# A two-block convolution network on one core: the second block's 3x3 convolution in tiles of four by four

## The chip, the cores and the metric

The kernel runs on one core of a Trainium2 chip. The time is that of one launch on the device, in microseconds (us); the median of several runs is given, and one further execution is profiled. The engines work side by side, each through its own queue in order, and wait for one another by semaphores: PE multiplies matrices (its weight loads are shown as PEld), DVE and ACT work element by element, POOL does a little, and SP issues most transfers. All data are 32-bit floats.

## What is computed

Eight images of 512 channels and 32 by 32 pixels pass two layers, each behind a group norm and added to its input. The first layer holds nearly all the work. Cut to what matters:

```python
t = cbs(x, cv1_w, cv1_bn, 0)            # 1x1, 512 -> 512
ys = [t[:, :C], t[:, C:]]               # C = 256
for i in range(N):                      # two blocks
    yi = ys[-1]
    z = cbs(yi, m_cv1_w[i], m_cv1_bn[i], 1)      # 3x3, 256 -> 256
    z = bot_attention(z, m_qkv_w[i], m_rw[i], m_rh[i])
    z = jax.nn.silu(bn_eval(conv2d(z, m_cv2_w[i], 0), m_cv2_bn[i]))
    ys.append(yi + z)
return cbs(jnp.concatenate(ys, axis=1), cv2_w, cv2_bn, 0)   # 1x1, 1024 -> 512
```

Here cbs is convolution, batch norm and SiLU. The attention has four heads of 64 channels over the 1024 pixels, with learned position terms added to the keys. The second layer is a depthwise 3x3 convolution (nine taps for each channel), ReLU, a threshold for each channel, a 1x1 convolution 512 to 512, ReLU and a threshold. The change concerns the 3x3 convolution of the second block.

## The kernel before, in words

**Pieces and lists.** Each step of an image is cut into small pieces, put under short names in a table (`add`, line 306), and four written lists say in which order the pieces are issued (`go`, line 309): FIRST (line 45) for image 0, then for each later image HEAD (line 63) followed by TAIL (line 79), or by LAST (line 85) for image 7. A list thus runs from one image into the next: HEAD begins with the 1x1 convolution of its own image (c, y) and also ends the second layer of the image before (o, O with ok, ou, oa and their capitals; fr, f). As every engine but POOL is bound to program order (`InOrder`), a list fixes the order on PE, DVE, ACT and SP.

**The names used below.** In a block: d, P, Rc, R, B, E, Ez are the 3x3 convolution; k, ka, kd, q, qa, v, va make keys, queries and values; s, e, p, w are the steps of attention (scores, exponentials, running sums, values), h, z, n, nr, ns, sc its end (n sums on PE, nr the reciprocal, ns eight transfers that spread it over the channels, sc the rescaling of z); m, ma, mr are the closing 1x1 convolution with its residual. o and O are products of the 1x1 convolution of the second layer, t the depthwise taps, Q the products of the last 1x1 convolution of the first layer, r0 to r3 sums of its right sides. ta, ti and to, in FIRST alone, transform the 3x3 weights once and write them to DRAM; rl and `ring_load` read them back.

**The 3x3 convolution** (`conv3`, line 737, used for both blocks) is done by a Winograd method in tiles of four columns by two rows: 6 by 4 = 24 products for each tile of eight outputs, in place of 72. The image is stored by column phase (x modulo four), padded, in `yp` (line 194). On DVE, `along_rows` (line 758) combines the columns and `across_rows` (line 786) the rows, which gives for each of three pairs j of column components four row components of 512 elements (128 channels of a half, in kr, vt and qy, which are free then). `products` (line 803) multiplies: for each j and each half m of the outputs, one piece P of 4 x 2 x 2 matmuls, 128 by 128 weights with 128 moving columns:

```python
for c in (1, 2, 0, 3):
    for i in range(2):
        at = place[c] * 256 + i * P
        for k in range(2):
            nc.tensor.matmul(
                flat(ps)[:, at : at + P],
                u[:, i, c, k, :],
                component(j, c)[:, (2 * i + k) * P : (2 * i + k + 1) * P],
                start=(k == 0), stop=(k == 1),
            )
```

Rc (ACT) copies one component out of PSUM, R (`rows_back`, line 822) turns the four components back on DVE, reading the rest from PSUM, B and E (lines 845, 865) do the columns, and Ez (line 870) applies the batch norm and SiLU into z.

**Weights and buffers.** A piece P takes one tile of 1 MB from the ring of `NRING` = 5 buffers (line 147) and asks for the next load at its end. Tiles of all kinds go through the ring in the order of use (`ring_sources`, line 387): for one block of a later image two tiles for o and O (or for cv1), six u tiles of the convolution, the qkv weights. A tile of o or O stays until its seventh product is done. Temporary tiles of 1024 elements come from a pool of `NWORK` = 11 (line 145).

Of the kernel before, what the change touches and what calls it, by code (L numbers as in the profile page):

```python
# [10 lines left out]
F32 = mybir.dt.float32  # L11
# [16 lines left out]
PITCH = F // 4 + 1  # L28
NWORK = 11
# [17 lines left out]
    ca ta2*2 c rl ca ta1*3 ti2 ti1 to1 d ti1 d y ya to1 ti1 y ya ti2 to2 d ti2 d to2 rl d*2 y ya  # L47
    y ya P*2 Rc R Rc d dw d*3 R d*2 P Rc P*3 Rc R B*2 R B Rc R E Ez B Rc R E Ez ta0 k*3 ka kp k X
    ka q*4 ta0*2 qa*2 v ti0 to0 ta1*2 to0 s e ti0*2 kp ta1 v va v*2 va ti1 s ti1*2 w s*2 e*2 w s
    e*2 p*3 w s*2 p ta2 e w*2 to1 e s*2 w p*2 s e p e w to1 e w ta2 s h p z e ta2 s e w*2 p s*2  # L50
    ti2 e*2 p w to2*2 s e s w*2 e p w*2 ti2*2 s*2 e*2 w p*2 s*2 w h e w s e w s e p s w s e*2 p*5
    n nr p z rh ns e p nc sc s e w*2 s*2 w*2 e*2 s w s*2 w h s z w sc e*4 w p*4 s w*2 e w p*2 w
    nc p n dp h z S nr nc*2 ns sc*2 Q m ma K mr m ma m*2 ma*2 mr*2 Q K mr d*7 P*2 Rc R d P Rc R
    Rc d*2 R d P Rc d R B*2 P Rc R E B P Rc Ez R B E Ez k cw rk X k*3 ka kp ka kp cw*3 v*2 va v*2
    va q rk q qa q cw s e cw q qa s e p w s*2 e p e p w cw s*2 dx w e p s e p e s e p*2 w*3 s e w
    g s e w h z s*2 e w s e w s g*2 s w p s*2 e*2 cw e cw w*2 e s p*2 w*2 s*2 cw w p*2 e p e*3 rk
    p cw*2 h p s z e s e w s e w rk p g p w*2 p w s n p nr s*2 e ns p*2 sc e w e nc s*2 g*3 e w s
    e*2 s e p w h s e nc w s e g p*3 w*3 p*2 w*3 sc w p h z*2 Q S n nr nc ns sc Q gm m ma mr sc
    m*3 ma*2 mr*2 ma mr Q u Q A x gd u Q A x gv i gp nc i*3 Q im id Q iv ip ib b gb A x bm i ga*4
    t i t*3 ct Q ct Q A x i*2  # L60
# [3 lines left out]
    c*4 ck cu ct*2 ca cu t im c cu*2 c*2 id iv cu y ca t cu*2 ca yk ca y*2 ip y t*2 d yu d ya y  # L64
    ib yu d*2 P d yu d*2 b P Rc R b bm d P d*2 y Rc R Rc b d R d B P Rc l B lr R B P Rc R E B P
    Rc R E Ez*2 yu bm*2 y lp yu ya yu*2 k t*19 v*2 va k*2 ya*2 ka k ka v*2 va X l kd q*2 qa lr lp
    t kd q s e t q qa s e p w s e s e p w*2 s*2 e*2 w s*2 w*2 s e*2 w s w e*2 s p*5 h e l w s*2 w
    e*2 lr t s w*2 p*2 e s e s e t w s w*2 z e s*2 e w e s w s*2 h e p e w s*2 p*5 z w e*3 s*2 e
    t w e p*2 s*2 e*2 w*2 l lr w p ot s p*2 e p*3 lp w h z n nr nc ns p*2 w lp w s*2 w e s w*2
    e*2 w*3 p sc p sc nc S p ot h z n nr o ok o ns O Ok ou oa ot*2 O sc m sc ma m ma Ou Oa m mr  # L70
    ma m ma O o mr*3 Ou ou d o d ou o O*2 d*2 P Ou ou Ou d*2 o ou d Rc ou nc R oa d*2 Ou oa P Rc
    d nc O P R d*2 P Rc P R B Oa Rc P R Ou Oa B*2 Rc B Rc R E R E Ez*2 o O k*4 ou oa Ou Oa ka*2
    fr*3 v*2 va q*2 v*2 dp qa g va g q X kd f g f kd s e q qa fr f*2 dx s e w s*2 e w e s*2 w s*2
    e*4 p*2 w s g*3 p*3 g s w*2 e s w*2 e*2 s*2 w g h s w e*2 w p*4 s*2 w s*2 w p*2 s*2 e p w e*6
    p w*2 h s*2 e*2 z p*4 w p*2 s e s z e w p*2 s n nr ns e w*4 nc s nc s e w p e w h s*2 w sc w
    e w s*2 e*3 w s p e p sc p*4 w*4 z n h z nr S ns
# [3 lines left out]
    r2 r0 Q*3 r0 sc*2 r0*2 m*2 r1 m ma gm m nc gd ma gv r1 ma r3 mr*2 K mr r2 r3 gp r2 ma mr r1  # L80
    gb ga r1 K ga ct r2 Q r3 Q*4 u1 u0 r3 Q u0*4 Q u0 Q a1 Q a0 x0 a0 ga x0 i a0 x0 i*3 im u0 a0
    id x1 ga ct Q iv ip Q u1 x0 ib b i u1 i bm t u1 t Q*2 u1 t*2 u1*2 a1 x1 a1*2 x1*2 i*2 nc
# [3 lines left out]
    Q*2 nc sc m sc nc rg m*3 ma*3 mr ma mr*3 Q A Q x i*2 im id Q iv ip Q ib Q A x b bm i*2 t*2 im  # L86
    id Q iv t*2 ip t*2 ib t b bm t*2 Q A x i*2 t Q l lr lp t im id t Q A iv ip t Q ib b bm t*4 x
    t A x t i*2 l lr o*2 t im id o iv t lp ip t ib o*2 rg b bm t*4 l lr t lp t*5 l lr lp o*20 oa
    o oa o*6 fr f oa*2 fr f oa*2 fr f oa*2 fr f
# [34 lines left out]
def fast_kernel(  # L124
# [54 lines left out]
    def load(dst, b):  # L179
# [14 lines left out]
    yp = [const_tile([P, 4, 2, F, PITCH], f"yp{l}") for l in range(2)]  # L194
# [9 lines left out]
        [dram.tile([P, 2, 4, 2, P], F32, tag=f"u{l}_{i}", name=f"u{l}") for i in range(6)]  # L204
        for l in range(2)
# [44 lines left out]
    for t in yp:  # L250
        nc.gpsimd.memset(t, 0.0)
# [5 lines left out]
    sc12 = const_tile([P, 4], "sc12")  # L257

    def fold_norms():
# [11 lines left out]
        nc.vector.tensor_scalar(sc12, sc[:, BN2 : BN2 + 4], -1.0 / 12.0, None, ALU.mult)  # L271
# [26 lines left out]
    def inner(t, m):  # L298
        return t[:, :, m, :, : F // 4]
# [19 lines left out]
    PAIRS = ((1, 2), (3, 4), (0, 5))  # L319

    def transform_weights(l, outer_queue):
# [26 lines left out]
        def store(j, c, t, queue=nc.sync):  # L348

            for m in range(2):  # L350
                src = t.rearrange("p (i m x) -> p i m x", i=2, m=2)[:, :, m]
                dst = u_dram[l][2 * j + m][:, :, c].rearrange("p i k o -> p i (k o)")
                queue.dma_start(dst, src)
# [16 lines left out]
        def outer_rows(j, c, dy):  # L370
            t = planes.pop((j, dy))
            nc.scalar.mul(t, t, 2.0)
            store(j, c, t, outer_queue)

        return (
            [[lambda j=j, dy=dy: along_rows(j, dy) for dy in range(3)] for j in range(3)],
            [[lambda j=j, i=i: inner_rows(j, i) for i in range(3)] for j in range(3)],
            [
                [lambda j=j, c=c, dy=dy: outer_rows(j, c, dy) for c, dy in ((0, 0), (3, 2))]
                for j in range(3)  # L380
            ],
# [5 lines left out]
    def ring_sources():  # L387
        for b in range(B):
            for l in range(2):
# [3 lines left out]
                for i in range(6):  # L393
                    yield u_dram[l][i].rearrange("p a b c d -> p (a b c d)"), 2048
# [288 lines left out]
    def cv1(order):  # L683
# [17 lines left out]
        def first_end(m):  # L701
            act(inner(yp[0], m - 2), by_phase(flat(open_.pop(m))), AF.Silu, BN0 + m)
# [21 lines left out]
    def quartered_cv1():  # L724
# [4 lines left out]
        def end(ps, p, low, n):  # L729
            m = 2 * p + low  # L730
            dst = inner(yp[0], low) if p else phases(y0[:, m, :])
            act(dst[:, :, n * 16 : n * 16 + 16], by_phase(ps), AF.Silu, BN0 + m)
# [4 lines left out]
    def conv3(l):  # L737
# [3 lines left out]
        yf = yp[l].rearrange("p r k h t -> p (r k h t)")  # L741
# [128 lines left out]
        def close(m):  # L870
            n = 2 * l + m
# [5 lines left out]
                scale=sc12[:, n : n + 1],  # L877
# [15 lines left out]

    def positions(l, m):
# [5 lines left out]
        nc.vector.tensor_tensor(phases(t), col.to_broadcast(full), row.to_broadcast(full), ALU.add)  # L900
        nc.sync.dma_start(r_dram[l][:, m], t)

    def qkv(l, by_input):


        wt, tiles, values = [], {}, {}
# [6 lines left out]
        def products(m, k):  # L913
            w = weights()
            if m not in tiles:
                tiles[m] = big_tile("ps_qk")
            for n in range(2):
                nc.tensor.matmul(
                    tiles[m][:, n, :],
# [8 lines left out]
        def keys(m):  # L928
            nc.scalar.copy(kr[:, m, :], flat(tiles.pop(m + 2)))
# [5 lines left out]
        def columns(m):  # L935
# [3 lines left out]
                phases(flat(tiles.pop(m + 2))),  # L939
# [4 lines left out]
        def lines(m):  # L944
            row = rh[:, l, m, :].unsqueeze(1).unsqueeze(3)
# [21 lines left out]
        def query_end(m):  # L967
            nc.scalar.copy(qy[:, m, :], flat(tiles.pop(m)))
# [925 lines left out]
```

## Time and profile before

| | us |
|---|---|
| median of three runs | 2582.23 (2579.84 to 2583.25) |
| the profiled execution | 2582.45 |
| its span | 2580.4 |
| PE, attention (ps_s and ps_av) | 518.6 + 518.3 busy |
| PE, both 3x3 convolutions (ps_c) | 119.8 + 118.1 + 117.0 busy |
| PE, ps_qk | 232.8 busy |
| PE, second layer and first 1x1 (ps_q from pt) | 176.8 busy |

The names of a row are the output, then the inputs, as the program calls them: ps_c is the output of a P (from kr, vt or qy, after j), ps_q of an o, O, c or y, ps_m of an m, ps_dn of an n, ps_s and ps_av of an s and a w. After the shapes comes the number of records; behind the bar stand the busy time of the group, the mean length of one in ns, and the idle time of the engine before it, with what ended it. The profiler writes two MATMUL and two LDWEIGHTS records for one 32-bit product. "128*32" is the part of the array that a product takes (rows * columns). All lines carry L103, the line of the helper that issues every instruction, so groups are told apart by tiles.

### The profile page before, as it was taken

The page shows a single profiled execution, that of the slowest core. Times are in us where ns is not written, and L with a number is a line of the kernel's source. Part 1 is how long each engine was busy: PE and PEld are TensorE (multiplying, and loading weights), DVE is VectorE, ACT ScalarE, POOL GpSimd, SP SyncE. Part 2 cuts the span into 40 slices and gives each one's busy share as a digit, 9 for nine tenths or more (in the row PEclk, how much of TensorE's full clock was granted, in tenths as well). Part 3 has the DMA queues.
Part 4 walks back from the last instruction along what each step waited for, and adds up shares of the span by engine and source line. Part 5 has one row for each costly group of instructions (what it writes and reads, how often), then busy time and mean ns, then how long its engine had stood idle before and what let it go on. Part 6 is the DMA issues. An engine that isn't in the chain of part 4 may idle for free.

```text
span 2580.4 us, 38500 instructions
## 1 busy us (share of the span) xinstructions
PE 2533.9 (98%) x15518; PEld 1329.0 (52%) x15518; DVE 2073.5 (80%) x2992; ACT 1207.6 (47%) x1595; POOL 126.2 (5%) x100
## 2 busy tenths in 40 slices
PE   7998999999999999999999999999999999999997
PEld 5463464644646346463464634646455554656443
DVE  8877599866988779886798868988699876998647
ACT  3634347353472634635355353644436454373524
POOL 1000000000000000000000000000000000000000
PEclk9999999999999999999999999999999999999999
DMA  9347141341414324052240612407033160322400
GB/s 351 127 165 264 50 155 34 109 160 59 150 31 147 117 72 141 32 184 80 73 147 17 222 43 80 139 18 247 30 110 96 50 214 32 139 66 83 127 17 34
DMA packets 116393, 284.38 MB, mean 110 GB/s; under 512 B 10608, under 2 KB 76400, under 8 KB 101872
## 3 DMA queue, kind: packets, MB, share of 16 engines
q1 hardware_dynamic: 108624, 263.76, 29.3%
q0 software_dynamic: 4032, 14.68, 3.1%
q10 hardware_dynamic: 3552, 3.41, 0.4%
q8 instruction: 124, 2.03, 0.3%
q14 instruction: 61, 0.50, 0.1%
HBM read 226.24 MB, written 38.80 MB: 103 GB/s over the span
## 4 chain that ended last, share of the span: by engine, by line
PE 72%; DVE 19%; DMA 3%; ACT 2%; issue 2%; SPq 1%; ACTq 0%; POOL 0%; DVEq 0%
PE ps_s L103 15%; PE ps_av L103 14%; PE ps_qk L103 8%; PE ps_c L103 7%; PE ps_q L103 7%; PE ps_cv L103 6%; PE ps_cv2q L103 6%; PE ps_m L103 4%; PE ps_v L103 4%; DVE ht L103 3%; DVE mid L103 2%; DVE sum L103 2%; SPq L103 1%; DVE y L103 1%; DVE vtmp L103 1%
## 5 line engine op out<-in xcount | busy, mean ns | idle before, releaser
L103 ACT ACTIVATE e<-ps_s 128x1024 f32<-128x1024 f32 x512 | 504.9, 1024 | 238.3 <-PE ps_s L103 194.7
L103 PE MATMUL ps_s<-qy,kr 64*64 64x512 f32 x4096 | 518.6, 592 | 7.7 <-ACT e L103 7.6
L103 PE MATMUL ps_av<-e,vt 64*64 64x512 f32 x4096 | 518.3, 593 | 0.0
L103 DVE TENSOR_TENSOR sum<-sum,e 128x1024 f32<-128x1024 f32 x384 | 468.5, 1220 | 58.3 <-ACT e L103 31.0
L103 DVE SCALAR_TENSOR_TENSOR ht<-xn,v_sb,ht 128x961 f32<-128x961 f32 (+1 forms) x256 | 319.3, 1252 | 8.4 <-ACT ht L103 3.1
L103 PEld LDWEIGHTS ps_av<-e,vt 64*64 64x64 f32 x4096 | 185.1, 133 | 254.3 <-issue 227.5
L103 PEld LDWEIGHTS ps_s<-qy,kr 64*64 64x64 f32 x4096 | 172.2, 132 | 278.6 <-issue 131.3
L103 PE MATMUL ps_qk<-z,wring 128*128 128x512 f32 x512 | 232.8, 598 | 2.3 <-ACT z L103 1.9
L103 PE MATMUL ps_q<-pt,wring 128*128 128x512 f32 x392 | 176.8, 594 | 0.0
L103 DVE TENSOR_TENSOR sum<-e 128x1024 f32<-128x1024 f32 x64 | 78.1, 1221 | 107.4 <-ACT e L103 67.8
L103 ACT COPY c<-ps_c 128x256 f32<-128x256 f32 x96 | 35.9, 374 | 260.8 <-PE ps_c L103 254.5
L103 PEld LDWEIGHTS ps_qk<-z,wring 128*128 128x128 f32 x512 | 94.6, 190 | 120.0 <-issue 99.6
L103 PEld LDWEIGHTS ps_c<-vt,wring 128*128 128x128 f32 x1024 | 118.9, 194 | 10.2 <-issue 10.2
L103 PEld LDWEIGHTS ps_c<-kr,wring 128*128 128x128 f32 x1024 | 117.9, 192 | 11.4 <-issue 8.1
L103 PE MATMUL ps_c<-vt,wring 128*128 128x128 f32 x1024 | 119.8, 277 | 3.3 <-DMA wring<-u 3.3
L103 PE MATMUL ps_v<-wring,z 128*128 128x256 f32 x512 | 117.9, 381 | 0.7 <-DVE kr L103 0.3
L103 PE MATMUL ps_c<-kr,wring 128*128 128x128 f32 x1024 | 118.1, 275 | 0.1
L103 PE MATMUL ps_c<-qy,wring 128*128 128x128 f32 x1024 | 117.0, 275 | 0.0
L103 PEld LDWEIGHTS ps_c<-qy,wring 128*128 128x128 f32 x1024 | 115.6, 192 | 0.0
L103 PE MATMUL ps_m<-z,wm_sb 128*128 128x512 f32 x256 | 113.9, 594 | 0.0
L103 PEld LDWEIGHTS ps_q<-pt,wring 128*128 128x128 f32 x392 | 71.7, 190 | 81.0 <-issue 69.4
L103 ACT ACTIVATE m<-ps_m,bi,sc 128x512 f32<-128x512 f32 x64 | 50.0, 781 | 134.7 <-PE ps_m L103 133.6
(189 smaller groups left out, 3299.5 us busy)
## 6 DMA issues: line engine op xcount, KB each, us to landing
wring<-u SPq DMA_DIRECT2D x96, 1024.0 KB, 4.8
wring<-q SPq DMA_DIRECT2D x28, 896.0 KB, 4.7
pt<-in_x SPq DMA_DIRECT2D x32, 512.0 KB, 11.4
rw<-r SPq DMA_DIRECT2D x256, 64.0 KB, 2.0
xt<-in_x SPq DMA_DIRECT2D x32, 512.0 KB, 6.5
out<-xt SPq DMA_DIRECT2D x32, 512.0 KB, 7.3
kr<-r POOLq DMA_DIRECT2D x28, 512.0 KB, 5.9
wring<-in_wqkv SPq DMA_DIRECT2D x16, 768.0 KB, 4.3
```

The costliest lines, as they stand in the source:

```text
L103: made = method(*args, **kwargs)
```

## The change

The second block's convolution is computed in tiles of four by four: 6 by 6 = 36 products for each tile of sixteen outputs, where two tiles of four by two took 48. The first block keeps `conv3`. What moves:

- The input of the second block's convolution is stored by row phase and tile in two tensors `yp1`, and with it the order of the pixels in the second block: keys, positions and queries of that block follow it, and residuals, right sides of the last 1x1 convolution and the r1, r2, r3 sums that touch it are made in two halves.
- On DVE a new piece dr (`by_rows`, eight steps for each half n of the column phases) combines the rows first; d (`along_rows`, three steps for each j) the columns.
- P is nine pieces for six. Each makes four units of 128 output channels, as 32 matmuls of 128 by 64 weights with 64 moving columns; the two 64-column halves follow each other.
- Rc copies two pieces of P at once (1024 elements; the last 512), and R reads the copy, in two steps for each (j, m).
- The weights of the second block become nine tiles of 1 MB for six, each loaded once for every image through the same ring; `more_rows` makes six sums for each j where `inner_rows` made three.
- All four lists are in another order, with the new pieces in them.

Cut to its core (lists: the second convolution in FIRST, whose lines before are left out, and in HEAD):

```diff
+    e p w*3 z n nr w*2 dx ns w*3 sc*3 h z sc nc S m*2 ma*2 mr*2 dr*8 m*2 ma*2 mr*2 dr*8 d dp Q*2
+    K*2 d*4 P d*2 P*3 Rc R P d*2 Rc R cw R*2 g nc R P*2 Rc R P Rc R*2 B*3 P Rc R*2 E Ez R*2 B E
+    Ez g rk X k*4 ka kp ka kp cw*3 rk cw v cw*2 v va v*2 va q*2 qa q s e q qa s e p w s*2 e*2 p w
...
 HEAD = """
...
-    e*2 w*3 p sc p sc nc S p ot h z n nr o ok o ns O Ok ou oa ot*2 O sc m sc ma m ma Ou Oa m mr
-    ma m ma O o mr*3 Ou ou d o d ou o O*2 d*2 P Ou ou Ou d*2 o ou d Rc ou nc R oa d*2 Ou oa P Rc
-    d nc O P R d*2 P Rc P R B Oa Rc P R Ou Oa B*2 Rc B Rc R E R E Ez*2 o O k*4 ou oa Ou Oa ka*2
-    fr*3 v*2 va q*2 v*2 dp qa g va g q X kd f g f kd s e q qa fr f*2 dx s e w s*2 e w e s*2 w s*2
...
+    p ns sc s*2 e w p e w p*2 w*2 S h n nr z sc ot*2 ns nc sc o ok o ou O m*2 Ok ma*2 mr o sc m
+    mr dr ou dr*3 oa m dr*3 ma*2 mr*2 dr*2 o O ou dr Ou dr*6 Oa O Ou d*3 o O ou O P*3 Ou*3 Oa Rc
+    d*3 ou oa d*2 R o P Rc nc R*3 nc d R ou P*2 Rc R oa R*2 O P*2 B P o O dp B*2 Rc R*2 E Rc R*2
+    B E Ez*2 Ou q k*2 ka q qa v q*2 qa v va kd ou Ou X k oa fr g s e g*2 k ka v*2 Oa*2 kd f fr*2
...
-    yp = [const_tile([P, 4, 2, F, PITCH], f"yp{l}") for l in range(2)]
+    yp0 = const_tile([P, 4, 2, F, PITCH], "yp0")
+    yp1 = [const_tile([P, 4, 4, ROWS], f"yp1_{n}") for n in range(2)]
+    vrows = const_tile([P, 6, 8, HD], "vrows")
...
     u_dram = [
-        [dram.tile([P, 2, 4, 2, P], F32, tag=f"u{l}_{i}", name=f"u{l}") for i in range(6)]
-        for l in range(2)
+        [dram.tile([P, 2, 4, 2, P], F32, tag=f"u0_{i}", name="u0") for i in range(6)],
+        [dram.tile([P, 4, 2, 2, P], F32, tag=f"u1_{i}", name="u1") for i in range(9)],
...
+        def more_rows(j, step):
+            first, mid, last = (planes[j, dy] for dy in range(3))
+            if step in (0, 3):
+                t = box[j] = work_tile("ucomp")
+                if step == 0:
+                    tt(t, first, last, ALU.add)
+                else:
+                    stt(t, last, 4.0, first, ALU.mult, ALU.add)
+            elif step in (1, 4):
...
+        def by_rows(n, step):
...
+            if step == 0:
+                stt(ab.rearrange("p (g x) -> p g x", x=HD), low, -4.0, high, ALU.mult, ALU.add)
+            elif step == 1:
+                tt(o[1], b, a, ALU.add)
+            elif step == 2:
+                tt(o[2], b, a, ALU.subtract)
...
+                stt(o[3], d[0], 2.0, d[2], ALU.mult, ALU.add)
+            elif step == 6:
+                stt(o[4], d[0], -2.0, d[2], ALU.mult, ALU.add)
+            else:
+                i0, i1 = (
+                    i.rearrange("p s (g x) -> p s g x", x=HD) for i in (parts[:, 0:4:3], parts[:, 1:3])
+                )
+                stt(both, i0, -4.0, i1, ALU.mult, ALU.add)
...
+        def along_rows(j, step):
...
+            if step == 0 and j < 2:
+                v = vrows.rearrange("p s (h g) x -> p h s (g x)", h=2)
+                out = zf.rearrange("p (s x) -> p s x", s=6)
+                if j == 0:
+                    stt(out, v[:, 0], -4.0, v[:, 1], ALU.mult, ALU.add)
+                else:
+                    tt(out, v[:, 1], v[:, 0], ALU.subtract)
+            elif step == 0:
+                v = vrows.rearrange("p s (r k) (i t) -> p r s (k i) t", r=4, t=n8)
+                a, b = (t.rearrange("p s (q t) -> p s q t", t=n8) for t in (p, q))
+                e = n8 - 1
+                tt(a[:, :, :, 1:], v[:, 1, :, :, 1:], v[:, 3, :, :, :e], ALU.subtract)
+                nc.scalar.copy(a[:, :, :, 0], v[:, 1, :, :, 0])
+                tt(b[:, :, :, :e], v[:, 0, :, :, 1:], v[:, 2, :, :, :e], ALU.subtract)
+                nc.scalar.mul(b[:, :, :, e], v[:, 2, :, :, e], -1.0)
+            elif j == 0:
+                tt(p if step == 1 else q, high, low, ALU.add if step == 1 else ALU.subtract)
+            elif j == 1:
+                s = 2.0 if step == 1 else -2.0
+                stt(p if step == 1 else q, low, s, high, ALU.mult, ALU.add)
+            elif step == 1:
+                stt(p, p, -4.0, high, ALU.mult, ALU.add)
+            else:
+                stt(q, low, -4.0, q, ALU.mult, ALU.add)
+
+        def products(j, part):
...
+            for x in range(4):
+                row = UNITS[4 * part + x][1]
+                for i in range(2):
+                    at = x * P + i * HD
+                    for k in range(2):
+                        from_ = ((i * 6 + slot[row]) * 2 + k) * HD
+                        for o in (0, HD):
+                            nc.tensor.matmul(
+                                ps[o : o + HD, at : at + HD],
+                                u[:, x, i, k, o : o + HD],
+                                comps[j][:, from_ : from_ + HD],
+                                start=(k == 0),
+                                stop=(k == 1),
+                            )
+            ring_load()
...
+        def rows_copy(n):
+
+            t = copies[n] = work_tile("c1")
+            if n < 4:
+                nc.scalar.copy(t, flat(banks.pop(n)))
+            else:
+                nc.scalar.copy(t[:, :512], banks.pop(n)[:, 0, :])
...
+        def rows_back(j, m, step):
...
+                tt(sd[:, :256], c[:, :256], c[:, 256:512], ALU.add)
+                tt(sd[:, 256:512], c[:, :256], c[:, 256:512], ALU.subtract)
+                return
...
+            stt(o[:, :, 0], s2, -0.25, s1, ALU.mult, ALU.add)
+            stt(o[:, :, 3], d2, -2.0, d1, ALU.mult, ALU.add)
+            stt(o[:, :, 1], d2, -0.5, d1, ALU.mult, ALU.add)
+            tt(o[:, :, 2], s1, s2, ALU.subtract)
+            e = o[:, :, 0:4:3]
+            outer = copied(j, 1)[:, 256 * m : 256 * m + 256].rearrange("p (y q x) -> p q y x", y=2, q=2)
+            tt(e, e, outer, ALU.subtract)
...
+        add("dr", *[lambda n=n, i=i: by_rows(n, i) for n in range(2) for i in range(8)])
+        add("d", *[lambda j=j, i=i: along_rows(j, i) for j in range(3) for i in range(3)])
+        add("P", *[lambda j=j, i=i: products(j, i) for j in range(3) for i in range(3)])
+        add("Rc", *[lambda n=n: rows_copy(n) for n in range(5)])
+        add("R", *[lambda j=j, m=m, i=i: rows_back(j, m, i) for j, m in jm for i in range(2)])
...
         def residual(n, m):
-            r = slice(2 * n, 2 * n + 2)
-            dst = inner(yp[1], m) if l == 0 else phases(qy[:, m, :])
-            nc.vector.tensor_tensor(dst[:, r], phases(ts[n, m]), inner(yp[l], m)[:, r], ALU.add)
+            for r in range(2):
+                t = ts[n, m][:, r * 256 : (r + 1) * 256]
+                if l == 0:
+                    own = lines(inner(m)[:, 2 * n + r])
+                    t = lines(t.rearrange("p (h t) -> p h t", h=F))
+                    nc.vector.tensor_tensor(by_line(padded(m, n, r)), t, own, ALU.add)
+                else:
+                    dst = lines(phases(qy[:, m, :])[:, 2 * n + r])
+                    nc.vector.tensor_tensor(dst, tiles(t), by_line(padded(m, n, r)), ALU.add)
...
-                    nc.tensor.matmul(
-                        ps[:, n, :], w[:, k, :], rhs(k, n), start=(k == start), stop=(k == stop)
-                    )
+                    parts = rhs(k, n)
+                    size = 512 // len(parts)
+                    for r, t in enumerate(parts):
+                        o = ps[:, n, r * size : (r + 1) * size]
+                        nc.tensor.matmul(
+                            o, w[:, k, :], t, start=(k == start and r == 0), stop=(k == stop)
+                        )
...
-            nc.vector.tensor_tensor(o[c], x[c], y[c], ALU.subtract)
+            three = o[c], x[c], y[c]
+            if any(isinstance(t, list) for t in three):
+                for r in range(2):
+                    nc.vector.tensor_tensor(*[of_column(t, r) for t in three], ALU.subtract)
+            else:
+                nc.vector.tensor_tensor(*three, ALU.subtract)
...
         for l in range(2):
-            conv3(l)
+            (square_conv3 if l else conv3)()
```

## The prediction

> **What bounds the kernel now.** I read the page's busy table first, then the waits of TensorE (PE), then its timeline in one middle image, and last the rows of the operations that the change touches.
>
> ```profile
> span 2580.4 us, 38500 instructions
> PE 2533.9 (98%) x15518; PEld 1329.0 (52%) x15518; DVE 2073.5 (80%) x2992; ACT 1207.6 (47%) x1595; POOL 126.2 (5%) x100
> ...
> PE pm L103 <- DVE mv L103: 13.3, 5, 7.8
> PE ps_s L103 <- ACT e L103: 7.6, 4, 4.9
> ```
>
> A busy PE is not yet a PE at its peak, so the pitch has to be checked. The timeline of PE around the second convolution of one middle image (start, length, then what):
>
> ```profile
> 1101.39 10.46 PE L103 MATMUL ps_q<-pt,wring 128*128 128x512 f32 x24
> 1111.69 3.73 PE L103 MATMUL ps_c<-kr,wring 128*128 128x128 f32 x32
> 1115.27 1.88 PE L103 MATMUL ps_q<-pt,wring 128*128 128x512 f32 x4
> 1116.98 3.73 PE L103 MATMUL ps_c<-kr,wring 128*128 128x128 f32 x32
> 1120.56 1.88 PE L103 MATMUL ps_q<-pt,wring 128*128 128x512 f32 x4
> 1122.27 7.31 PE L103 MATMUL ps_c<-vt,wring 128*128 128x128 f32 x64
> 1129.42 7.31 PE L103 MATMUL ps_c<-qy,wring 128*128 128x128 f32 x64
> 1136.57 3.60 PE L103 MATMUL ps_q<-ht,wring 128*128 128x512 f32 x8
> ```
>
> From start to start, 24 ps_q records take 10.30 us, 0.429 us each, and a piece P of 32 ps_c records takes 3.58 us, 0.112 us each (every product leaves two records). No gap stands between the groups. The chain of waits has the same piece at 1111.86 and at 1424.59, so an image takes 312.7 us, and PE is packed through it. PE is the bound; what leaves PE leaves the time, if the other engines keep up.
>
> **What the change needs from PE.** It uses half-width products (128 rows by 64 columns, 64 moving columns), which the trace of before does not show. The nearest are the four-way split ps_dn and the quadrants of attention:
>
> ```profile
> 129.88 0.61 PE L103 MATMUL ps_s<-qy,kr 64*64 64x512 f32 x4
> 130.42 0.81 PEld L103 LDWEIGHTS ps_dn<-sum,ones 128*32 128x32 f32 x32 [0.81 <-issue]
> 130.42 1.08 PE L103 MATMUL ps_dn<-sum,ones 128*32 128x128 f32 x32
> 131.43 0.66 PE L103 MATMUL ps_s<-qy,kr 64*64 64x512 f32 x4
> 1501.77 0.15 PEld L103 LDWEIGHTS ps_av<-e,vt 64*64 64x64 f32 x4 [0.28 <-issue]
> ```
>
> One ps_dn record lasts 0.273 us, so 32 of them start within 0.81 us: seven steps of about 0.112 us, four records in each. That is the pitch of one full 128-column record, so column tiles run side by side. Four 64-column weight loads, each 0.132 us long, take 0.15 us together, so loads into different tiles overlap too.
>
> The Trainium skill says the same in "TensorEngine Tiling (Array Packing)", Key Properties: tiles execute LdWeights and Matmul in parallel, and a change of tiling mode drains the array. The trace shows the drain: ps_s at 129.88 should be followed after 0.43 us and is followed after 0.54; ps_dn's eight steps of 0.112 should end 0.90 us after the start and ps_s follows after 1.01. I take 0.1 us for a change of mode. "TensorE: Matmul & The Clock Gate", LDWEIGHTS, says that a load costs by its columns: 192, 132 and 109 ns for 128, 64 and 32 columns here agree in direction, with a fixed part. The same page (Wait — 56ns, not 53.3ns?) gives a floor of about 25 ns from start to start; ps_dn's average of 0.81/32 = 25 ns is no lower, and the new products need 29.
>
> **PE, part by part.** Before: 6 pieces x 32 records x 0.1117 = 21.4 us for an image's second convolution. After: 9 pieces P x 4 components x 2 x 2 x 2 halves = 288 products, 576 records, 288 side-by-side pairs. Of the 0.1117 us, 0.1067 is the moving (512 columns take 0.429, so 128 take 0.107) and 0.005 is fixed; half the columns give 0.053 + 0.005 = 0.058. So 288 x 0.058 = 16.7 us. Bounds: 15.4 with nothing fixed, 18.4 if each of the four instructions of a pair costs 16 ns. The list HEAD has the nine P in three runs between products of full width: 6 changes of mode, 0.6 us. Net: 21.4 - 17.3 = 4.1 us less PE for an image.
>
> The third block's right sides in the last 1x1 convolution become two matmuls of 256 columns for one of 512. A 256-column record (ps_v, 16 in 3.45 us) takes 0.215, so two cost 0.43 as one did: nothing.
>
> **VectorE (DVE).**
>
> ```profile
> L103 DVE SCALAR_TENSOR_TENSOR v<-vtmp 128x512 f32<-128x512 f32 x64 | 41.2, 686 | 0.3
> L103 DVE TENSOR_TENSOR mid<-ps_c,c 128x256 f32<-128x256 f32 x96 | 40.3, 420 | 7.7 <-ACT c L103 6.9
> ...
> 1108.76 2.42 DVE L103 TENSOR_TENSOR kr<-v 128x512 f32<-128x512 f32 x4
> ```
>
> Back to back, operations overlap a little: four of 512 in 2.42 us, a pitch of 0.60; the 256 ones follow each other at 0.33, the 1024 ones at 1.13. So an operation occupies 0.07 us plus 1.04 ns per element: 0.20 for 128, 0.87 for 768, 0.77 for 672. Before, per image: d 12 x 0.60 + 6 x 0.60 + 6 x 0.57 = 14.2, R 24 x 0.33 = 7.9, B 5.1, E 1.2: 28.4 us. After: dr 2 x (4 x 0.60 + 4 x 0.33) = 7.5; d three of 768 for j=0 and for j=1 (2.6 each), two of 672 and two of 768 for j=2 (3.3), in all 8.5; R 6 x (2 x 0.33 + 4 x 0.20 + 0.33) = 10.8; B and E as before: 33.1 us. With the residuals and the t sums cut in two (8 more pieces of 256 for 4 of 512 at each layer, +0.5; six chunks, +0.4) DVE gains some 5.6 us an image. Over the image DVE has slack (80% busy); in this stage it has not.
>
> ScalarE: Rc goes from 6 x 0.374 to four copies of 1024 (1.01) and one of 512 (0.59): +2.4 us, and four small edge copies go. It is half idle there; nothing.
>
> **The stage in HEAD, in order.** Zero is the first o after attention 1. PE has 14 units of 1.72 us (o, O, m), 24.1 us, before the first P. The first m comes after three units at 5.2, its second half at 6.0; the rescaled z needs the rw transfers, half of which landed 5.0 us after the reciprocal before (1089.1 to 1094.1), so about 6.1, plus 0.6 for the product: a wait of 0.8 us. Before, four units stood there and it waited 0.3 at most. After the last m (14.5) DVE does mr, the rest of dr, O's sums and the three d of j=0, and is through at 24.9: P starts at about 25. From P on, PE has 9 x 1.87 + 0.6 + four o/O (6.9) = 24.3 us until it wants z. DVE has, from there, Ou 1.8, ou 1.2, d 5.9, R 10.8, B 5.1, E 1.2 = 26.0, waits some 2 us for the first copies of P2 to P3, and ends at about 28; the closing activation (1.25) follows. The first q needs half of z only and waits some 0.6 us, the second k 0.4: 1.0 us in all (0 to 3). So of 4.1 us, 0.5 + 1.0 = 1.5 to 1.8 go back to DVE; I take a net gain of 2.3 us for each of the seven images that HEAD serves: -16.
>
> Weights: nine tiles of 1 MB for six. Two of the five ring buffers are held by o and O, so six tiles come while P runs.
>
> ```profile
> 1115.00:1120.00 5.00, 5.00 (x36) 4.04 (x36) 5.00 (x11) 2.42 (x7) 0.00 (x0) 1.00 0.61 210
> 1145.00:1150.00 5.00, 5.00 (x20) 3.53 (x19) 2.10 (x4) 1.01 (x1) 1.73 (x2) 1.00 1.02 357
> ```
>
> (The last number is GB/s.) The queues give 357 at most, 2.95 us for a tile, 17.7 us for six, against 17.4 from P3's load to P8 in my order: the last P can be up to 2 us late, hidden by the two o/O after it while DVE is later still. Without that cover it costs these 2 us.
>
> **First and last image.** In FIRST nothing stands beside P: PE saves 4.5 us there, but waits 5.8 us for R, B, E after the last P where it waited 1.9: -0.6. The weight transforms take nine more sums of 1024 (+10 us DVE, before and in attention 1, where DVE's gaps, 3.7 and 2.1 us the longest, hold most): +2 (0 to 5). LAST touches no conv stage: 0 (plus or minus 3). Other lists change order only; PE stays packed there, as it was.
>
> **Sum.** -16 - 0.6 + 2 = -15. From the profiled execution's own 2582.45 us (span 2580.4, 2.0 outside it) 2567; the median before is 2582.23, so it is the same reference: 2567 us.
>
> **Rivals.** (A) My case, PE gain half given back to DVE: 2555 to 2577, chance 0.47. (B) The order hides DVE after all, and its waits: 8 x 4.1 = 33 less 2, about 2550 (down to 2540 with the lower pair price); for it, that DVE's waits are my hand sum's; against, DVE's 26 us beside PE's 24.3. Chance 0.20. (C) The other side: the chain dr, d, R, B, E, on DVE with Rc and the weight tiles late, becomes the bound of the stage. If it gives back more than 4.1 us in an image the kernel is slower; at 7 us (three more in the chain from small strided operations, two from tiles) it is 8 x 2.9 = +23, about 2605. For it, windows of the stage already show DVE at 5.00 of 5.00 us; against, slack in front of P. Chance 0.22, part of it near zero. (D) The half tiles do not run side by side: 576 x 0.058 = 33.4 us, +12 an image, 2680. ps_dn speaks against it: 0.03. The remaining 0.08 is an intro or end that loses what the middle gains: no change.
>
> Within 0.2% (5 us) I call no change. Faster 0.68, same 0.10, slower 0.22. Range 2540 to 2595; A's own range stands above.
>
> **What would show it.** P pieces of 64 records at 1.87 us (right) or 3.7 (D); in the chain, waits of the first q or k for ACT z of 0.5 to 1.5 us an image (A), none (B), several (C); the period of an image at 310.4. A P that waits for DMA wring<-u would show the weights late. A pair price above 0.068 us or a wait for z above 3 us breaks the forecast.

## The result, and the profile after

| | before | after |
|---|---|---|
| median | 2582.18 us | 2595.77 us (2592.64 to 2605.7) |
| ratio | | 1.0058, 95% interval 1.0046 to 1.007 |
| profiled execution, its span | 2582.45, 2580.4 us | 2595.85, 2594.0 us |

The kernel is slower by 13.6 us; 2567 was forecast, with 2540 to 2595 as the range.

The page of the changed kernel, in the order in which the one before was read: span and busy times, then the chain of waits by engine.

```profile
span 2594.0 us, 45160 instructions
PE 2511.4 (97%) x18750; PEld 1282.9 (49%) x18750; DVE 2147.5 (83%) x3268; ACT 1237.6 (48%) x1569; POOL 137.3 (5%) x107
...
PE 81%; DVE 9%; DMA 5%; ACT 1%; issue 1%; SPq 1%; POOL 0%; DVEq 0%; ACTq 0%; POOLq 0%
```

PE's busy time fell by 22.5 us, of 33 in the sum's PE part (8 x 4.1), and the span still grew by 13.6: PE now stands idle, which it hardly did. What for, the waits of PE say (total us, times, the longest):

```profile
PE ps_c L105 <- DMA wring<-u: 19.6, 21, 3.1
PE ps_c L105 <- issue: 11.6, 7, 2.9
...
PE ps_qk L105 <- ACT z L105: 2.5, 3, 1.9
```

Before, the first line was one wait of 3.3 us in the first block, and the second did not exist. Of the 19.6 us, 3.1 are again that wait in the first block; the rest is new. The third line is DVE's chain ending late, which was forecast at 1.0 us an image: it is nearly absent. The same middle image that the prediction showed:

```profile
1109.78 7.03 PE L105 MATMUL ps_q<-pt,wring 128*128 128x512 f32 x16
1117.04 0.45 PE L105 MATMUL ps_c<-kr,wring 128*64 128x64 f32 x8 [0.23 <-DVE kr L105]
1117.91 5.58 PE L105 MATMUL ps_c<-kr,wring 128*64 128x64 f32 x184 [0.42 <-DVE kr L105]
1123.42 1.98 PE L105 MATMUL ps_q<-pt,wring 128*128 128x512 f32 x4
1125.34 2.08 PE L105 MATMUL ps_c<-vt,wring 128*64 128x64 f32 x64
1128.38 2.08 PE L105 MATMUL ps_c<-vt,wring 128*64 128x64 f32 x64 [0.95 <-DMA wring<-u]
1130.82 2.08 PE L105 MATMUL ps_c<-vt,wring 128*64 128x64 f32 x64 [0.36 <-DMA wring<-u]
1132.84 1.98 PE L105 MATMUL ps_q<-pt,wring 128*128 128x512 f32 x4
1135.14 2.08 PE L105 MATMUL ps_c<-qy,wring 128*64 128x64 f32 x64 [0.32 <-DVE c L105]
1138.06 2.09 PE L105 MATMUL ps_c<-qy,wring 128*64 128x64 f32 x64 [0.83 <-DMA wring<-u]
1140.65 2.08 PE L105 MATMUL ps_c<-qy,wring 128*64 128x64 f32 x64 [0.51 <-DMA wring<-u]
1142.66 3.70 PE L105 MATMUL ps_q<-ht,wring 128*128 128x512 f32 x8
```

The three P of kr run through at 1.9 us each, as forecast; from the fourth on, four of six wait for their tile, 2.65 us in this image. The gap of 0.32 us at 1135.14, put down to DVE, is of the same kind: the tile of this P landed at 1135.0. (So are two waits of other images, put down to ACT, 1.8 and 1.1 us.) No gap comes after 1142.66: k needs no wait for z. From the first P to the first k pass 29.2 us, where the old stage took 28.3. In images 4 and 7 it takes 31.9 and 32.3. Now the queues, by windows of that stage (the length, the busy time of PE, its weight loads, DVE, ACT and POOL, the granted clock, and last the busy share of the queues and GB/s), and the list of transfers issued there:

```profile
1116.00:1118.00 2.00, 1.35 (x12) 0.41 (x12) 1.98 (x3) 0.00 (x0) 0.00 (x0) 1.00 0.00 0
1118.00:1140.00 22.00, 19.53 (x512) 16.50 (x512) 21.39 (x49) 6.50 (x12) 0.00 (x0) 1.00 0.83 303
1122.00:1124.00 2.00, 2.00 (x54) 1.69 (x51) 1.97 (x4) 0.74 (x1) 0.00 (x0) 1.00 0.99 414
```

```profile
1119.80 13.47 SPq L105 DMA_DIRECT2D wring<-u  x6
wring<-u SPq DMA_DIRECT2D x6, 1024.0 KB, 7.4
```

The queues are idle until the first P has begun, as all buffers are full or held; then six tiles are asked for, each at the end of a P, and take 7.4 us to land (median; 4.8 over the whole kernel before). The first, asked for at 1119.80, takes 4.7 us, the others 6.6 to 7.6; the sixth is asked for at 1132.95 and lands at 1140.5, just before the last P starts. Three free buffers are three P, 5.8 us, of look-ahead.

The second line of the waits, issue, is of another kind. In image 0 it stands inside the P, where no buffer changes hands. PE's weight loads there, and the queues in one window of 0.2 us (188.0 to 188.2) at the start of the first of the long gaps:

```profile
185.04 2.93 PEld L105 LDWEIGHTS ps_c<-vt,wring 128*64 128x64 f32 x96
190.61 2.82 PEld L105 LDWEIGHTS ps_c<-vt,wring 128*64 128x64 f32 x94 [2.63 <-issue]
...
196.26 3.81 PEld L105 LDWEIGHTS ps_c<-qy,wring 128*64 128x64 f32 x128 [1.84 <-issue]
201.65 1.01 PEld L105 LDWEIGHTS ps_c<-qy,wring 128*64 128x64 f32 x32 [1.57 <-issue]
```

```profile
q1 hardware_dynamic: 10, 0.08, 97.0%
q8 instruction: 1, 0.02, 28.9%
```

Gaps come 128 records apart, with 256 PE instructions between them (a weight load and a product each), and the page's queue q8, named instruction, moved 149 packets and 2.44 MB in this run: 16.4 KB each, 252 PE instructions for each. Its packets begin at 188.2, 193.8 and 199.3, and PE goes on at 190.61, 196.26 and 201.65, 2.3 to 2.5 us after each. The Trainium skill has the mechanism ("Runtime: NRT & Kernel Launch", Instruction fetch mechanics): an engine's instructions are refilled in blocks of 16 KiB, 256 of them, through a DMA queue that its sequencer drives. It calls the cost of a block boundary mostly hidden. Here it is not: 256 instructions last 3.9 us in these P, where an old P had 64 of them in 3.58 us (256 in 14.3), and the queues are full of weights. After a gap the next packet begins only some 3 us later, and from one restart to the next pass 5.4 to 5.7 us. The skill also says ("DMA: Bandwidth & Descriptors", Queues, rings and completion order) that an engine of the DMA takes turns between queues packet by packet, so that such a packet waits among the weights' packets; the share of 97% for q1 agrees, the turns themselves no run shows.

So theory W: the weight tiles come too late, for want of look-ahead and of queue time; with it F, PE's instructions come too late through the same queues. Rival D: DVE's longer chain (dr, d, R) holds the stage. Rival H: the half-width products are slower than they look.

### The profile page after: what moved, and what is told of

Its sections match the earlier page's. It is cut to its first block, busy times and chain, and to the rows that moved or that the text cites. A ratio compares the mean times of both kernels' runs of the same rounds, so it can differ in the third digit from the quotient of the medians.

```text
span 2594.0 us, 45160 instructions
## 1 busy us (share of the span) xinstructions
PE 2511.4 (97%) x18750; PEld 1282.9 (49%) x18750; DVE 2147.5 (83%) x3268; ACT 1237.6 (48%) x1569; POOL 137.3 (5%) x107
## 3 DMA queue, kind: packets, MB, share of 16 engines
q1 hardware_dynamic: 115344, 292.07, 31.9%
q8 instruction: 149, 2.44, 0.4%
## 4 chain that ended last, share of the span: by engine, by line
PE 81%; DVE 9%; DMA 5%; ACT 1%; issue 1%; SPq 1%; POOL 0%; DVEq 0%; ACTq 0%; POOLq 0%
PE ps_s L105 16%; PE ps_av L105 15%; PE ps_c L105 10%; PE ps_q L105 9%; PE ps_cv2q L105 8%; PE ps_qk L105 8%; PE ps_cv L105 7%; PE ps_v L105 4%; DMA wring<-u 4%; PE ps_m L105 3%; PE ps_dn L105 1%; DVE vtmp L105 1%; DVE vrows L105 1%; DVE ht L105 1%; DVE kr L105 1%
## 5 line engine op out<-in xcount | busy, mean ns | idle before, releaser
L105 PEld LDWEIGHTS ps_av<-e,vt 64*64 64x64 f32 x4096 | 158.2, 133 | 277.9 <-issue 272.3
L105 ACT COPY c<-ps_c 128x256 f32<-128x256 f32 (+2 forms) x88 | 55.0, 624 | 287.1 <-PE ps_c L105 280.3
L105 PE MATMUL ps_c<-vt,wring 128*64 128x64 f32 (+1 forms) x2048 | 109.6, 237 | 24.8 <-DMA wring<-u 14.2
L105 PEld LDWEIGHTS ps_c<-vt,wring 128*64 128x64 f32 (+1 forms) x2048 | 106.2, 152 | 35.8 <-issue 14.1
L105 PE MATMUL ps_c<-qy,wring 128*64 128x64 f32 (+1 forms) x2048 | 109.1, 239 | 9.4 <-DMA wring<-u 5.4
L105 DVE TENSOR_REDUCE keep<-pw 128x1 f32<-128x1024 f32 x30 | 36.4, 1213 | 96.5 <-ACT pw L105 96.5
L105 PEld LDWEIGHTS ps_c<-qy,wring 128*64 128x64 f32 (+1 forms) x2048 | 106.0, 154 | 15.7 <-issue 6.8
L105 PEld LDWEIGHTS ps_v<-wring,z 128*128 128x128 f32 x512 | 96.4, 190 | 34.2 <-issue 14.5
L105 PEld LDWEIGHTS ps_c<-kr,wring 128*64 128x64 f32 (+1 forms) x2048 | 104.0, 151 | 17.4 <-DVE kr L105 15.3
L105 PE MATMUL ps_c<-kr,wring 128*64 128x64 f32 (+1 forms) x2048 | 107.3, 236 | 4.9 <-DVE kr L105 4.5
```

The lines of the kernel that those rows point to most:

```text
L105: made = method(*args, **kwargs)
```

## The experiments

The medians are of 4 to 21 executions, but e7 and e8 were executed once; ratios are to the kernel before on the same chip. The waits are those of one execution, which can lie some 4 us off the median (e9 and e12 below it, e2 above). The first of the three numbers holds, where the profile puts it down so, the wait in the first block too: 3.1 us in the change and in e12, 4.6 in e1, 3.8 in e8.

| run | median us | ratio, 95% interval | PE's waits in the profile: wring<-u / issue / ACT z, us |
|---|---|---|---|
| after | 2595.77 | 1.0058 (1.0046 to 1.007) | 19.6 / 11.6 / 2.5 |
| e1_half_u | 2571.48 | 0.9957 (0.994 to 0.9973) | 6.4 / 3.9 / 7.5 |
| e2_dve_light | 2593.28 | 1.0048 (1.0036 to 1.006) | 15.4 / 13.0 / 4.2 |
| e3_half_u_dve | 2562.19 | 0.9927 (0.991 to 0.9943) | 1.4 / 4.4 / 5.1 |
| e4_before_split | 2586.06 | 1.0014 (1.0007 to 1.0022) | 0 / 0 / 2.4 |
| e5_order | 2584.02 | 1.0003 (0.9995 to 1.001) | 0 / 18.2 / 4.4 |
| e6_order_dp | 2583.28 | 1.0002 (0.9993 to 1.001) | 0.4 / 18.8 / 3.6 |
| e7_third_u | 2578.23 (once) | | 0 / 2.5 / 11.7 |
| e8_full_width | 2673.4 (once) | | 3.8 / 0 / 2.2 |
| e9_spread | 2584.89 | 1.0008 (0.9999 to 1.0016) | 0.2 / 5.8 / 12.1 |
| e10_spread_early | 2594.85 | 1.0055 (1.0041 to 1.0068) | 0 / 7.5 / 12.3 |
| e11_spread_last | 2582.13 | 1.0003 (0.9995 to 1.0011) | 0.4 / 9.0 / 12.1 |
| e12_spread_dve | 2578.26 | 0.9992 (0.9984 to 1.0) | 4.7 / 8.8 / 8.2 |

### Half the weight bytes, half of DVE's d, both

```diff
-yield u_dram[l][i].rearrange("p a b c d -> p (a b c d)"), 2048
+size = 1024 if l else 2048
+yield u_dram[l][i].rearrange("p a b c d -> p (a b c d)")[:, :size], size
...
-u[:, x, i, k, o : o + HD],
+u[:, x % 2, i, k, o : o + HD],
```

```diff
-stt(out, v[:, 0], -4.0, v[:, 1], ALU.mult, ALU.add)
+stt(out[:, :3], v[:, 0, :3], -4.0, v[:, 1, :3], ALU.mult, ALU.add)
```

The second is done in the same way to all operations of d. What is left out makes the block's result wrong, so all three kernels also make its scale tiny.

> The changed kernel with the nine weight tiles of the second convolution loaded to half (512 KB each, not 1 MB); units 2 and 3 of a P use the weights of units 0 and 1, and the batch norm scale is made tiny, so that the numbers are not the reference's. PE, DVE and ACT do the same work. Theory W (the weight tiles come too late for P: 3.1 us of waits in a middle image, more in images 0, 4 and 7): 2563 to 2580 us, no wait of ps_c for DMA wring<-u left, stage from the first P to the first k 27 us or less instead of 29.2. Theory V (the DVE chain dr, d, R, B, E bounds the stage): 2590 to 2597, as the changed kernel.

> The changed kernel with the d pieces of the second convolution computed for half of their rows only (about 5 us less DVE work in an image; the other half is stale, scale tiny as in e1). Weights as in the changed kernel. Theory W: within 4 us of the changed kernel, 2590 to 2597, the waits for wring<-u as long as before. Theory V: 2560 to 2580.

> Both of the above at once: weight tiles of half size and half of d. Theory W with DVE next in line: 5 to 12 us below e1 (2555 to 2570), since the wait for z that appears once weights are early goes too. If DVE has no part even then: within 3 us of e1. Theory V: as e2.

The stage with half the bytes, on PE:

```profile
1113.52 5.58 PE L105 MATMUL ps_c<-kr,wring 128*64 128x64 f32 x184 [0.41 <-DVE kr L105]
1119.03 1.98 PE L105 MATMUL ps_q<-pt,wring 128*128 128x512 f32 x4
1120.95 5.82 PE L105 MATMUL ps_c<-vt,wring 128*64 128x64 f32 x192
1126.70 1.98 PE L105 MATMUL ps_q<-pt,wring 128*128 128x512 f32 x4
1128.61 5.82 PE L105 MATMUL ps_c<-qy,wring 128*64 128x64 f32 x192
1134.36 3.70 PE L105 MATMUL ps_q<-ht,wring 128*128 128x512 f32 x8
1139.05 3.70 PE L105 MATMUL ps_qk<-z,wring 128*128 128x512 f32 x8 [0.99 <-ACT z L105]
```

Of the work nothing but the bytes differs (the tiny scale stands in e2 too, which gains little), and 24.3 us go, to below the kernel before. From the first P to the first k: 26.4 us. No wait for weights was expected to be left; in the second block three are, 1.8 us in all. In place of the gaps comes the wait for z that had been forecast, 0.99 us and then 0.18. Cutting DVE alone gives 2.5 us and leaves the waits for weights and instructions standing (28.4 us of them); the same cut on top of half the bytes gives 9.3. W holds; D is next in line, not first.

### The kernel before, with half-width products

```diff
-nc.tensor.matmul(flat(ps)[:, at : at + P], u[:, i, c, k, :], ...)
+for o in (0, HD) if l else (None,):
+    rows_ = slice(None) if o is None else slice(o, o + HD)
+    nc.tensor.matmul(flat(ps)[rows_, at : at + P], u[:, i, c, k, rows_], ...)
```

> The kernel before with each ps_c matmul of the second block cut into two halves of 64 output columns (128 by 64 weights, 128 moving columns): twice the PE instructions in a P, the same weights bytes and DVE work. If half tiles run side by side and instructions cost nothing: 2578 to 2586 us, P piece of 64 records in 3.5 to 3.8 us. If the two halves run one after the other: a P of 7.1 us, 2740 us. Theory F (fetching PE instructions holds PE up): gaps inside a P that nothing explains (issue), a few us for an image, 2590 us or more.

```profile
1117.91 3.71 PE L103 MATMUL ps_c<-kr,wring 128*64 128x128 f32 x64
1121.56 1.98 PE L103 MATMUL ps_q<-pt,wring 128*128 128x512 f32 x4
1123.47 7.21 PE L103 MATMUL ps_c<-vt,wring 128*64 128x128 f32 x128
1130.51 7.16 PE L103 MATMUL ps_c<-qy,wring 128*64 128x128 f32 x128
1137.60 2.84 PE L103 MATMUL ps_q<-ht,wring 128*128 128x512 f32 x6
```

A P of twice as many records takes 3.52 to 3.65 us, start to start, where it took 3.58 undivided: halves run side by side. What the division costs are the changes of mode: the unit between two P takes 1.91 us for 1.71. The stage is 0.5 us longer, 8 x 0.5 = 4 us, and the run is 3.65 slower. H falls, and so does rival (D) of the prediction.

### One tile more ahead, and the input's loads elsewhere

The weights left whole. e5 puts all seven o in front of the P, so that one buffer less is held:

```diff
-... Oa O Ou d*3 o O ou O P*3 Ou*3 Oa Rc d*3 ou oa d*2 R o P Rc ... R*2 O P*2 B P o O dp
+... Oa O Ou d*3 o ou o*2 P*3 ou*3 oa*3 Rc d*3 d*2 R O P Rc ... R*2 O P*2 B P O*2 dp
```

> The change, with one thing in another order in HEAD: all seven products o of the first quarter stand before the nine P, and four products O of the second quarter take their places between and after the P (the sums and closings follow their products). PE has the same work, and the same number of units stand before, between and after the P; but only one of the five ring buffers is then held by a tile of O, where o and O held two, so one weight tile more is loaded ahead. Theory (weight tiles late for want of look-ahead): four tiles are there at the first P and the other five come at 2.7 us each in the 17 us until they are needed; the waits for DMA wring<-u fall from 19.6 us to under 7, the stage takes 26 to 27 us from the first P to the first k as with half the bytes, and the time is 2568 to 2580 us. Rival (the bytes themselves are too many for the queues, whatever is loaded ahead): the wait moves to the last P or to the tiles of k and v, and the time stays at 2588 to 2596. Rival (DVE has become the bound): a wait for ACT z takes the place of the saved time; 2588 to 2596.

e6 has also, in FIRST, dp out of `d dp Q*2 K*2` and into `w*2 dp dx ns`.

> The run before, and in FIRST the piece dp (the loads of the next image's input, 2 MB on the same queue) is moved from right in front of image 0's nine P of the second block to the end of its first attention. If image 0's late weight tiles and its gaps inside the P come from the load on the queues, its stage (25.9 us from the first P to the first k with the change) becomes 1 to 3 us shorter, and the time lies 1 to 4 us below the run before. If they have another cause, both are the same within 1 us.

The same image with e5:

```profile
1115.62 4.76 PE L105 MATMUL ps_c<-kr,wring 128*64 128x64 f32 x155 [0.42 <-DVE kr L105]
1121.36 1.04 PE L105 MATMUL ps_c<-kr,wring 128*64 128x64 f32 x29 [0.97 <-issue]
1122.33 1.98 PE L105 MATMUL ps_q<-pt,wring 128*128 128x512 f32 x4
1124.24 5.95 PE L105 MATMUL ps_c<-vt,wring 128*64 128x64 f32 x192
1130.12 1.98 PE L105 MATMUL ps_q<-pt,wring 128*128 128x512 f32 x4
1132.03 4.79 PE L105 MATMUL ps_c<-qy,wring 128*64 128x64 f32 x153
1138.09 1.38 PE L105 MATMUL ps_c<-qy,wring 128*64 128x64 f32 x39 [1.27 <-issue]
```

One tile of look-ahead ends every wait for a weight tile and gives 11.8 us with all the bytes, half of what halving them gave. It was to give 16 to 28: the instructions now come late in the middle images too, in the midst of a P, 18.2 us in all where it was 11.6. What the weights no longer hold back, the fetch does. e6 missed: image 0's stage, from the first P to the first k, takes 25.8 us, within the 24.9 to 29.1 of the other runs with all the bytes and these P, and the time is the same within 1 us. Nothing shows the input's loads as its cause; why the fetch is late in image 0 even in e7 stays open.

### A third of the weight bytes; full width

e7 reads only every third tile and uses it for all three P of a component (rh, which lets the ring load these tiles in image 0, stands later in FIRST for it); e8 makes one product of each pair of halves:

```diff
-for o in (0, HD):
-    nc.tensor.matmul(ps[o : o + HD, at : at + HD], u[:, x, i, k, o : o + HD], ...)
+nc.tensor.matmul(ps[:, at : at + HD], u[:, x, i, k, :], ...)
```

> The change, but only every third weight tile of the second block's convolution is loaded, and the three P of a component all use that one (the products of two tiles in three are made with wrong weights, so the output is not the reference's; the block's scale is set to 1e-9 to keep the numbers small). PE's instructions are the same, 256 in 4 us in this stage, while the weight bytes fall to a third. If PE's waits marked issue inside the P come from instructions that are fetched through queues full of weights, none over 0.3 us stands inside a P of image 0, and the waits of ps_c for issue fall from 11.6 us to under 2. If the fetch itself is too slow for 256 instructions in 4 us, gaps of 1 to 3 us stay in image 0 at every 128 records. The time is 2562 to 2572 us either way.

> The change, but each pair of half-width products (64 columns of weights each, same moving data) is made as one product of 128 columns with 64 moving columns: the same result from half the matmuls and weight loads. If a load of 128 columns costs its own time whatever moves (0.19 us long, about 0.11 us from start to start), a P of 32 records takes about 3.6 us, no P waits for weights any more, and the time is 2596 + 72 x 1.6 - 7 x 3 = about 2690 us. If the moving data alone set the pitch, P takes 1.9 to 2.1 us as in the change, and the time is 2580 to 2596.

e7's waits of PE, as far as they concern the stage:

```profile
PE ps_qk L105 <- ACT z L105: 11.7, 16, 3.0
...
PE ps_c L105 <- issue: 2.5, 1, 2.5
```

With the same instructions at the same pace, the seven gaps become one (in image 0, so the forecast of none was not quite met), and all middle images have none. Its time missed, at 2578 for 2562 to 2572: attention 1 of image 0 took 7 us longer in this execution (74.5 us for 67.5 from the first s to the first m), with one wait of 5.2 us for ACT e, ahead of the stage, where rh had been moved; whether by that was not tried. In e8

```profile
1147.10 10.48 PE L105 MATMUL ps_c<-kr,wring 128*128 128x64 f32 x92 [0.21 <-DVE kr L105]
```

92 records take 10.32 us to the next start, 0.112 each, as with 128 moving columns: half the moving data gains nothing. That the weight load of 128 columns sets the pitch agrees with this, as two loads of 64 do better. Only the split makes the change's 36 products cheap. The time is 17 us under the forecast, which had left out that the 11.6 us of gaps go too. At that pace, with as many weight bytes, no gap marked issue is left; but the bytes are spread over more time too, so e8 alone does not part the two. e7 shows that the bytes matter, e9 below that the pace does. That the fetch is what is late rests on these, on the distance of 256 instructions and on the packets of q8. The fetch's own request is not in the trace.

### The O spread among the P

```diff
-P*3 ou*3 oa*3 Rc d*3 d*2 R O P Rc ... P*2 Rc R R*2 O P*2 B P O*2 dp
+P*2 ou*3 oa*3 O P Rc d*3 d*2 R P O Rc ... P*2 Rc R R*2 O P*2 B P O dp
```

> The order with o in front, with the four O spread: P P O P P O P P O P P P O for P P P O P P P O P P P O O. Work, bytes and look-ahead are the same, and a pair of P (256 PE instructions) then has 5.6 us instead of 3.9 in the first three of its places; two more changes of mode cost 0.2 us for an image. If the gaps marked issue are PE's instructions arriving too slowly beside the weights, their sum falls from 18 us to under 8, and the time from 2584 to 2570 to 2578 us, below the kernel before. If they come from the queues' load alone whatever PE's rate, they stay at 15 to 20 us and the time at 2582 to 2587. If DVE takes over, waits for ACT z grow by what the gaps lose.

> The run before, with the last o also ahead of the last O in front of the P, so that the fourth weight tile is asked for one unit (1.7 us) sooner, when the queues are idle; one DVE sum more (0.6 us) stands in front of the first P. Fewer bytes then come beside the P: the gaps fall by another 1 to 4 us in all, and the first P of an image may start up to 0.6 us later (4 us in all). 2568 to 2578 us; the same as the run before within 3 us.

```profile
PE ps_qk L105 <- ACT z L105: 12.1, 16, 2.2
...
PE ps_c L105 <- issue: 5.8, 5, 2.0
```

The gaps fell from 18.2 to 5.8 us (9.0 and 8.8 in e11 and e12, with the same order), as F has it, and the waits for z rose from 4.4 to 12.1, as the last sentence of the expectation has it: DVE has taken over, and the median did not move. e10 missed: it was to equal e9 and is 10 us slower. Its first P starts 1.2 us late for d, after ACT had held an O by 0.36, so that the way from the end of attention to the first P grew from 24.5 to 26.1 us in each image. Work put in front of the P is on the path.

### Is it DVE now, and what LAST costs

> The run with the four O spread, with the list LAST as it stood before the change: the same pieces in the old order. If the new order of LAST costs the 1 to 3 us by which the end after the last attention is longer than before, the time is 1 to 3 us below the run it starts from (2584.9), about 2582; if the end is longer for another reason, the two are the same within 1 us. Nothing in the images before is touched.

> The run with the four O spread, with the operations d on half of their slots (three of six; half of the components are left at what was in the buffer, so the output is not the reference's, and the block's scale is 1e-9): some 4 to 5 us less DVE for an image. If DVE has taken over as what ends the stage once weights and instructions come in time, the waits of ps_qk for ACT z fall from 12.1 us to under 6 and the time by 5 to 9 us, to 2576 to 2580; in the change as it was, the same cut gave 2.5. If the waits for z come from somewhere else, they stay over 9 us and the time stays at 2583 to 2587.

The cut in d now takes the median 6.6 us down; by the ratios it is about 4, in the change as it was about 2.6, and the intervals of the ratios do not part these two. What shows DVE at the end of the stage in e9 are the waits: those for z fell from 12.1 to 8.2, less than forecast, and the 4.5 us that the first P of the images waited for d are gone.

LAST stays open. e11's median is 2.8 us lower, by the ratios about 1.3, and the intervals overlap. From the end of the last attention to the end of the kernel pass 109.9 us in e11 and 110.3 in the kernel before; with the new list it is 113.7 in e9, but 111.1 in the change and 111.4 in e12. No run with its whole computation beat the kernel before; e5, e6, e9 and e11 equal it.

## Why the prediction was wrong

**The step that failed** is the last sentence on the weights: "the last P can be up to 2 us late, hidden by the two o/O after it while DVE is later still." Both halves failed. The lateness was sized on the best rate seen, 2.95 us a tile, 17.7 us for six against 17.4, and for the last P alone. Measured, the six took 20.7 us from the first request to the last landing. A tile asked for with idle queues took 4.7 us (the page of before had 4.8 as the median), those asked for behind it 6.6 to 7.6; so five P of the image shown wait, not the last alone. And nothing hid it: o/O stand behind the waiting P in PE's own queue and only move back with it. A wait on the engine that is the bound is hidden only if another engine would have held the end anyway; DVE would by 1.2 us (e1), not by the 3.0 of this image and more in others. What is more, the sentence "Without that cover it costs these 2 us" was put beside the sum, not in it.

**What no step had**: that PE's own instructions come through the queues and can be late, 11.6 us.

The other steps, each with what it measured:

- A pair of half-width products 0.058 us: 0.060 (184 records in 5.51 us), P 1.92 for 1.87; +0.5 us an image. Changes of mode 0.1 us each: confirmed (an O between two P takes 1.92 us, elsewhere 1.72).
- First P at 25 us: 24.5, after waits for d of 0.65 us. The wait of m for z of 0.8 us: none in the image shown.
- DVE's part: the first step of d for j = 0 and 1 has 1536 elements and takes 1.75 us, where 768 and 0.87 had been put in: +1.7 us an image. It changed nothing in the result, as DVE was not the bound.
- The wait for z of 1.0 us: 0.99 + 0.18 once the weights are in time (e1); in the change 2.5 us over all images.
- Net gain of 2.3 us for each later image: 2.5 in e1, measured between the ends of attention 2 in the middle images. In the change as it is, images 1 to 7 lose 10.3 us together (the lag at the end of the second attention grows from 2.4 to 12.7 us), 1.5 each. 7 x 3.8 = 27 us is nearly all of the miss of 28.8.
- Image 0: 1.4 us of loss forecast, 2.4 measured to the end of its second attention (1.6 in e9 and 7.4 in e11, where nothing in image 0 was changed). LAST: 0 plus or minus 3, and +0.9 in the change, +3.2 to 3.4 in e1, e5 and e9.
- Rival (C), the slower side, named the right place and gave it 0.22; of its price, 7 us an image with three of them DVE's, the weights' part was paid and DVE's was not.

That the change does on PE what it says (busy 22.5 us less), and that the other engines cover PE's part but for about 1.2 us, was right; e1, 4.5 us over the forecast, shows what the sum would have met.

## What to carry to other kernels

When PE's work shrinks and its weights grow, walk the loads through the list one by one: when is each buffer freed, when is its tile asked for, when needed. Put in the time from request to landing, not the best rate: a rate over the stage hides a late tile, and a wait on the engine that is the bound is paid in full unless another engine ends later still. Instructions are themselves fetched: where they become short, count them for each microsecond beside the transfers.

## What the runs showed of the hardware

- PE can stop at every 256th instruction when these last 3.9 us and the queues are full. The five gaps over 1 us that the change's profile marks issue last 1.4 to 2.9 us, and each ends 2.2 to 2.5 us after the start of a 16.4 KB packet of the instruction queue. With 256 instructions in 7.3 us (e4, fewer bytes) there was none. The page's figure for that queue, 0.4% of the span, gives no hint of it.
- The queues moved 414 GB/s over 2 us and 303 over the 22 us of the stage, where 357 had been taken from the trace of before as the most.
- With 128 columns of weights a record starts each 0.112 us, with 64 moving columns (e8) as with 128; with two halves of 64 columns side by side a pair starts each 0.060 us.
- A 1 MB tile landed in 4.7 us when it was asked for with idle queues, in 6.6 to 7.6 us behind others.
